# Eight dense chunks in every image group, six indirect transfers under way, reordered first loads, border taps without padding

## The chip, the core and the metric

The kernel runs on one core of a Trainium2 chip. A core has five engines that run side by side and meet only at semaphores: TensorE (PE in the profile; its weight loads are listed as PEld), VectorE (DVE), ScalarE (ACT), GpSimd (POOL) and SyncE (SP), and 16 DMA engines that all queues share. The metric is device time in microseconds from the start to the end of one execution. The kernel before the change takes 2309.76 us in the median of 14 runs (2300.69 to 2324.23 us).

## The reference, cut to what matters

The input is 32 images of 128 channels and 56 x 56 pixels (3136 tokens). Each image goes through a binary 3 x 3 convolution with padding 1, then a linear attention, then a mixture of 8 experts of which each token uses the best two.

```python
x = x + conv(sign(groupnorm(x)), sign(w)) * Alpha            # layer 0; w from M, Z and rv
t = to_tokens(x)
n = layernorm(t)
q, k, v = n @ Wq + bq, n @ Wk + bk, n @ Wv + bv
t = t + q * sum(k * v, axis=tokens)                           # attention
n = layernorm(t)
probs = softmax(n @ router_w + router_b)
top_p, top_i = top_k(probs, 2)                                # renormed to sum 1
t = t + sum_k top_p[k] * (n @ expert_w[top_i[k]] + expert_b[top_i[k]])
out = from_tokens(t)
```

## The kernel before

**Tiling of one image.** The 3136 tokens of an image are cut into 25 chunks of at most 128 (`n_ck`), and the chunks into blocks of four (`PER`, 512 tokens). The convolution of an image is seven tiles of eight image rows (`conv`, L597 to L608): nine taps accumulate in one PSUM tile of 8 x 56 = 448 columns, reading `xs`, a 58 x 58 bf16 copy of the signs with a border of zeros. After it come the turn to tokens (`to_tokens`, L628), the statistics, a Gram matrix (L703), a chain of eight small steps (`kv_1` to `kv_8`), the projection (`project`, L822) and the routing, most of it small DVE work.

**Two ways through the experts.** The first `DENSE[g]` chunks of an image are *dense*: a block is turned to channels (`to_channels`, L1078), and for each of the eight experts the gates of all tokens are broadcast by DMA over the partitions (`spread`, tile `bc`, L1096), multiplied in on DVE (`gated`, L1105, two experts at a time), and put through the expert on PE (`experts`, L1123, tile `ff`, with the expert biases by L1117). `finish` (L1134) adds, `store` writes out.

The other chunks are *sorted*. Each token is a row of 132 numbers; POOL writes the 128 rows of a chunk into a DRAM table sorted by the pair of experts they need (`scatter`, L1325, one indirect DMA a chunk). When all images of a group have scattered, lists of tiles are made (`list_1` to `list_4`), and for each *quad* of four tiles SP loads the rows (`tile_load`, L1617), PE turns them (`tile_turn`, L1624) and runs just the two experts of the tile (`tile_experts`, L1642), ACT scales both results out of PSUM (`tile_read`, L1660 and L1667), DVE adds (`tile_sum`, `tile_out`), and the result goes to DRAM (`tile_store`). Then POOL gathers each chunk's rows back (`gather`, L1400, one indirect DMA a chunk), PE turns a block of them (`back_turn`, L1415), ACT copies (`back_out`, L1423) and SP stores.

Images 0 to 27 are in four groups, `GROUPS = (8, 8, 8, 4)`, with `DENSE = (8, 8, 12, 12)` dense chunks an image; images 28 to 31 are dense in all 25 chunks. So the kernel runs 96 dense blocks, 428 scatters, 428 gathers and 132 quads.

**What limits the indirect transfers.** `in_turn` makes each indirect DMA wait until the one issued `IN_FLIGHT = 4` places earlier has landed. All scatters and gathers go through POOL in one order.

**The order of the work.** A planner (`in_order`) decides it. Every step is entered with `at(due, key, engine, work, ...)`: a due time, an engine, an estimate of its work, the steps it comes after, the buffers it takes and frees (`ROOM`), and `delay`, the time until what it started has landed. The planner plays the steps through on these estimates and emits them in the order found; PE, DVE and ACT then execute exactly that order, so a step that is late holds up everything behind it on its engine. For scatters and gathers the estimate is 2.0 on POOL, and a gather is taken to land after `GATHER_LANDS = 12.0`.

**The start.** SP issues the first image's load (`load_x`, L308 and L309) and then some 20 small loads of weights and biases (L322 to L335); ACT issues `rv`, `M` and the five `Z` (L318 to L321). DVE sums `M` and `Z` in five steps over all 1152 columns (L340), ACT takes the sign (L343, tile `w_bin`). These stand ahead of the planned steps. `gn_sum` (ACT, L547) sums the first image, `gn_total`, `gn_mean` (L560) and `gn_neg` make its mean, `gn_sign` (L567) writes `xs`, and the first convolution follows. `prepare` centres the weights after the first image's convolution. SP issues the loads of images 1 and 2 behind the small loads.

Of the kernel before, what the change touches and what calls it, by code (L numbers as in the profile page):

```python
# [48 lines left out]
AF = mybir.ActivationFunctionType  # L49
ALU = mybir.AluOpType  # L50
# [4 lines left out]
C = 128  # L55
GROUP = 4
TAPS = 9
K_REP = 5
N_EXP = 8
# [4 lines left out]
ROWS = 8  # L64
# [2 lines left out]
ROW = C + 4  # L67
N_PAIR = N_EXP * (N_EXP - 1) // 2
GROUPS = (8, 8, 8, 4)
DENSE = (8, 8, 12, 12)  # L70

IN_ORDER = {mybir.EngineType.PE, mybir.EngineType.DVE, mybir.EngineType.Activation}
NEWTON = 3
IN_FLIGHT = 4

GATE_LANDS, SPREAD_LANDS, STORE_LANDS, TILE_LANDS, GATHER_LANDS = 5.0, 6.5, 5.0, 6.0, 12.0
TILE_PACE = (0.7, 0.6, 0.4, 0.3)
GATHER_PACE = (1.0, 0.8, 0.5, 0.4)
N_Q = C + 2 * N_EXP
# [11 lines left out]
    x=3, tok=3, ps=5, acc=1, ff=2, y=3, qs=3, tt=4, bc=4, gt=2, gated=2,  # L91
# [86 lines left out]
def conv_attn_moe_kernel(  # L178
# [19 lines left out]
    nc = tc.nc  # L198
# [121 lines left out]
    for k in range(K_REP):  # L320
        nc.scalar.dma_start(z_sb[k], z_w[k].rearrange("i t o -> i (t o)"))  # L321
    nc.sync.dma_start(alpha_col, alpha.rearrange("c a b -> c (a b)"))  # L322
    nc.sync.dma_start(wq_sb, w_q)
    nc.sync.dma_start(wk_sb, w_k)
    nc.sync.dma_start(wv_sb, w_v)
    nc.sync.dma_start(bq_col, b_q.unsqueeze(1))
    nc.sync.dma_start(bq_bc, b_q.unsqueeze(0).to_broadcast([C, C]))
    nc.sync.dma_start(bk_bc, b_k.unsqueeze(0).to_broadcast([C, C]))
    nc.sync.dma_start(bv_bc, b_v.unsqueeze(0).to_broadcast([C, C]))
    nc.sync.dma_start(rw_sb, router_w)  # L330
    nc.sync.dma_start(rb_bc, router_b.unsqueeze(0).to_broadcast([C, N_EXP]))
    nc.sync.dma_start(ew_s.rearrange("d (e c) -> d e c", c=C), expert_w.rearrange("e d c -> d e c"))
    nc.sync.dma_start(eb_row, expert_b.rearrange("e c -> (e c)").unsqueeze(0))
    for r in range(9):
        nc.sync.dma_start(eb9[r * N_EXP : (r + 1) * N_EXP, :], expert_b)  # L335


    w_acc = z_sb[K_REP]
    for k in range(K_REP):
        nc.vector.scalar_tensor_tensor(  # L340
            w_acc, z_sb[k], rv_bc[:, k : k + 1], w_acc, ALU.mult, ALU.add
        )
    nc.scalar.activation(w_bin.rearrange("p t o -> p (t o)"), w_acc, AF.Sign)  # L343

    wv_bk = const.tile([C, C], F32, name="wv_bk")
    n_bkbv = const.tile([C, C], F32, name="n_bkbv")
# [174 lines left out]
    def plan_image(i: int):  # L521
# [15 lines left out]


        def load():
            d["x"] = load_x(i, nc.sync) if i else first_x  # L540

        def gn_sum(r0, r1):
            if r0 == 0:
# [22 lines left out]
        def gn_sign(r0, r1):  # L566
# [5 lines left out]
            )  # L572

        at(
            s - 60, ("load", i), "SP", 0.1, load,
            after=[("load", i - 1)] + ([("gn_sign", 0, GN_PARTS - 1)] if i == 1 else []),
            take=["x"], delay=13.0 if i else 19.0,
        )
        for j in range(GN_PARTS):
            rows = j * height // GN_PARTS, (j + 1) * height // GN_PARTS  # L580
# [15 lines left out]

        def conv(b):  # L597
            cv = ps.tile([C, ROWS, width], F32, tag="ps", name=f"cv_{i}_{b}")
            for t in range(TAPS):
                dy, dx = t // 3, t % 3  # L600
                nc.tensor.matmul(  # L601
                    cv,
                    lhsT=w_bin[:, t, :],
                    rhs=xs[:, b * ROWS + dy : b * ROWS + dy + ROWS, dx : dx + width],
                    start=(t == 0),
                    stop=(t == TAPS - 1),
                )
            d["cv", b] = cv  # L608

# [1211 lines left out]
```

## Time and profile before

| what | us |
|---|---|
| median of 14 runs | 2309.76 |
| the profiled execution | 2322.44 |
| its span | 2320.7 |
| PE busy | 2121.9 (91%), 12074 instructions |
| PE weight loads busy | 1458.3 (63%) |
| DVE busy | 1980.0 (85%) |
| ACT busy | 1528.0 (66%) |
| POOL busy | 1000.4 (43%) |
| DMA bytes | 448.56 MB, 193 GB/s mean |
| granted TensorE clock, mean | 0.963 |

Times below are from the start of the span of this one execution, which is 0.5% above the median. "Busy" of PE counts the stretches in which any matmul is under way; matmuls overlap, so the distance from one group's start to the next is the better price of a matmul. A row of a timeline or of the chain gives the start, the duration and the engine, line and tiles; in brackets stands the idle time before it and what ended it. A wait row says who waited for whom: total, times, longest.

### The profile page before, as it was taken

The numbers are of one execution on the slowest core, as the hardware profiler recorded it, in microseconds if no ns is written. First come the engines' busy times: TensorE is split into PE (matmuls) and PEld (weight loads), VectorE is DVE, ScalarE is ACT, GpSimd is POOL, SyncE is SP. The second block draws the span as 40 slices with busy tenths as digits, with TensorE's granted clock in tenths as the row PEclk, the third lists the DMA queues.
The fourth block names the chain that finished last, engine by engine and source line by source line (L and its number), as shares of the span: only waits on it lengthen the run. The fifth ranks groups of instructions, "written<-read, shape, count | busy, mean of one in ns | idle before, by whom it ended". The sixth has DMA issues, their size and how long they took to land. (4 is left out here: it accounts for less than half of the span.)

```text
span 2320.7 us, 45155 instructions
## 1 busy us (share of the span) xinstructions
PE 2121.9 (91%) x12074; PEld 1458.3 (63%) x12074; DVE 1980.0 (85%) x6360; ACT 1528.0 (66%) x4883; POOL 1000.4 (43%) x971
## 2 busy tenths in 40 slices
PE   4989899999999999889999999998889879999989
PEld 2656556666777776557667776655567655666644
DVE  3799999999999999898788989898678868778875
ACT  3766767668888887467867887555567846674311
POOL 1044444333332335554545454544545345534564
PEclk9999999999999999899999999999899989999999
DMA  4044454465665665457767876565666766877788
GB/s 166 29 138 159 161 178 154 138 180 180 187 174 178 179 182 184 135 168 235 214 184 228 257 212 205 183 213 171 213 207 197 229 170 197 266 227 236 233 281 304
DMA packets 317741, 448.56 MB, mean 193 GB/s; under 512 B 61066, under 2 KB 223154, under 8 KB 317491
## 3 DMA queue, kind: packets, MB, share of 16 engines
q1 hardware_dynamic: 289090, 386.97, 53.4%
q0 software_dynamic: 27392, 55.17, 7.9%
q10 hardware_dynamic: 1008, 3.54, 0.4%
q8 instruction: 102, 1.67, 0.3%
q14 instruction: 149, 1.21, 0.2%
HBM read 319.51 MB, written 126.00 MB: 192 GB/s over the span
## 5 line engine op out<-in xcount | busy, mean ns | idle before, releaser
L1325 POOL DMA_INDIRECT rows<-tok,row_no x428 | 501.2, 1171 | 786.7 <-ACT tok L1319 389.7
L1123 PE MATMUL ff<-gated,ew_d 128*128 128x512 f32 (+1 forms) x1536 | 721.9, 599 | 37.9 <-DVE gated L1105 25.1
L1400 POOL DMA_INDIRECT back<-res,res_no x428 | 489.7, 1144 | 518.4 <-PE back_ps L1415 171.4
L1105 DVE TENSOR_TENSOR gated<-tt,bc 128x1024 f32<-128x1024 f32 x384 | 450.2, 1177 | 96.5 <-PE ff L1123 46.5
L1123 PEld LDWEIGHTS ff<-gated,ew_d 128*128 128x128 f32 x1536 | 278.0, 195 | 278.5 <-issue 216.8
L601 PE MATMUL cv<-xs,w_bin 128*128 128x448 bf16 x2016 | 427.5, 361 | 9.5 <-ACT xs L567 4.2
L1660 ACT ACTIVATE v<-to,t_in 128x128 f32<-128x128 f32 x528 | 252.6, 478 | 122.7 <-PE to L1642 54.3
L601 PEld LDWEIGHTS <-w_bin 128*128 128x128 bf16 x2016 | 199.1, 100 | 188.1 <-issue 36.4
L1642 PEld LDWEIGHTS to<-ew_s,turned 128*128 128x128 f32 x2112 | 258.4, 193 | 49.3 <-issue 32.2
L1642 PE MATMUL to<-ew_s,turned 128*128 x2112 | 271.9, 278 | 18.2 <-issue 10.3
L836 ACT ACTIVATE qs<-q,r 128x136 f32<-128x136 f32 (+1 forms) x800 | 246.3, 407 | 54.2 <-PE q L822 33.7
L694 ACT ACTIVATE y<-tok,r 128x128 f32<-128x128 f32 (+1 forms) x800 | 252.5, 405 | 39.5 <-DVE r L512 21.4
L822 PE MATMUL q<-move,x 128*128 128x144 f32 (+1 forms) x1600 | 246.0, 301 | 23.2 <-issue 11.4
L822 PEld LDWEIGHTS q<-move,x 128*128 128x128 f32 (+1 forms) x1600 | 219.0, 197 | 54.3 <-issue 25.4
L703 PEld LDWEIGHTS gram<-y 128*128 128x128 f32 (+1 forms) x1600 | 198.6, 191 | 34.0 <-issue 22.2
L641 DVE BATCH_NORM_STATS2 st<-tok 128x6 f32<-128x128 f32 (+1 forms) x800 | 179.2, 277 | 42.3 <-ACT tok L634 34.3
L703 PE MATMUL gram<-y 128*128 128x129 f32 (+1 forms) x1600 | 210.5, 277 | 0.0
L1667 ACT ACTIVATE w<-to,t_in 128x128 f32<-128x128 f32 x528 | 205.6, 389 | 0.0
L856 DVE BATCH_NORM_STATS2 st<-tok 128x6 f32<-128x128 f32 (+1 forms) x800 | 194.8, 281 | 0.0
L634 ACT COPY tok<-xt 128x512 f32<-128x512 f32 (+1 forms) x224 | 117.6, 566 | 105.1 <-PE xt L628 51.8
L612 DVE SCALAR_TENSOR_TENSOR x<-cv,alpha_col,x 128x448 f32<-128x448 f32 x224 | 151.3, 676 | 32.7 <-PE cv L601 21.0
L1319 ACT ACTIVATE tok<-tok,a 128x128 f32<-128x128 f32 (+1 forms) x428 | 173.5, 436 | 0.1
(216 smaller groups left out, 2883.1 us busy)
## 6 DMA issues: line engine op xcount, KB each, us to landing
bc<-gp SPq DMA_DIRECT2D x368, 512.0 KB
x<-in_x_dram SPq DMA_DIRECT2D x64, 784.0 KB
t_in<-rows SPq DMA_DIRECT2D x528, 66.0 KB
res<-v SPq DMA_DIRECT2D x132, 256.0 KB
out_dram<-o SPq DMA_DIRECT2D x100, 256.0 KB
out_dram<-tt SPq DMA_DIRECT2D x92, 256.0 KB
rows<-zeros SPq DMA_DIRECT2D x116, 66.0 KB
rows<-tok,row_no POOLq DMA_INDIRECT x428
```

Source lines behind the costliest of these rows:

```text
L601: nc.tensor.matmul(cv, lhsT=w_bin[:, t, :], rhs=xs[:, b * ROWS + dy : b * ROWS + dy + ROWS, dx : dx + width], start=(t == 0), stop=(t == T ...
L694: nc.scalar.mul(y[:n, j, :C], d["tok"][:n, c, :C], d["r1"][:n, c : c + 1])
L703: nc.tensor.matmul(d["gram"], lhsT=y[:n, j, :C], rhs=y[:n, j, :], start=(c == 0), stop=(c == n_ck - 1),)
L822: nc.tensor.matmul(p[:n, k, :], lhsT=d["x"][:, c * C : c * C + n], rhs=move, start=True, stop=True,)
L836: nc.scalar.mul(qs[:n, k, : C + N_EXP], p[:n, k, : C + N_EXP], d["r1"][:n, c : c + 1])
L1105: nc.vector.tensor_tensor(g[:, :, :n], d["tt", b][:, :n].unsqueeze(1).to_broadcast([C, 2, n]), d.pop(("bc", b, k))[:, :, :n], ALU.mult,)
L1123: nc.tensor.matmul(d["ff", b][:, :n], lhsT=ew_d[:, e * C : (e + 1) * C], rhs=g[:, j, :n], start=False, stop=(e == N_EXP - 1),)
L1325: dma = nc.gpsimd.indirect_dma_start(out=groups[group]["rows"], out_offset=bass.IndirectOffsetOnAxis(ap=d["row_no"][:n, c - n_dense : c - ...
L1400: dma = nc.gpsimd.indirect_dma_start(out=d["back", c][:n, :], out_offset=None, in_=groups[group]["res"][: quads_of(group) * WIDE, :], in_o ...
L1642: nc.tensor.matmul(p[:, k, j, :], lhsT=t[:, n * C : (n + 1) * C], rhs=ew_s[:, bass.ds(d["cols", q][j][n], C)], start=True, stop=True,)
L1660: nc.scalar.activation(d["v", q][:, n, :], p[:, k, 0, :], AF.Identity, bias=row[:, C + 2 : C + 3], scale=row[:, C : C + 1],)
L1667: nc.scalar.mul(d["w", q][:, n, :], p[:, k, 1, :], row[:, C + 1 : C + 2])
```

## The change

`DENSE` becomes (8, 8, 8, 8): in the 12 images of the last two groups a third block of four chunks goes the sorted way. `IN_FLIGHT` becomes 6, the planner's estimate for a scatter or gather 1.5 in place of 2.0, and `GATHER_LANDS` 9.0 in place of 12.0. The convolution takes the centre tap first and each border tap only over the columns and rows where it meets the image, so the zero border of `xs` is no longer read. The weight sum is cut into three parts of 384 columns, it and the sign become planned steps, and the convolution waits for the last part (`("binary", 2)`). The small loads move from SP to POOL (`load_small`, a planned step), `prepare` waits for them, and the loads of images 1 and 2 move from SP to ACT.

```diff
-DENSE = (8, 8, 12, 12)
+DENSE = (8, 8, 8, 8)
...
-IN_FLIGHT = 4
-GATE_LANDS, SPREAD_LANDS, STORE_LANDS, TILE_LANDS, GATHER_LANDS = 5.0, 6.5, 5.0, 6.0, 12.0
+IN_FLIGHT = 6
+GATE_LANDS, SPREAD_LANDS, STORE_LANDS, TILE_LANDS, GATHER_LANDS = 5.0, 6.5, 5.0, 6.0, 9.0
...
-    nc.sync.dma_start(wq_sb, w_q)
...
-    for r in range(9):
-        nc.sync.dma_start(eb9[r * N_EXP : (r + 1) * N_EXP, :], expert_b)
+    def load_small():
+        nc.gpsimd.dma_start(wq_sb, w_q)
...
+        for r in range(9):
+            nc.gpsimd.dma_start(eb9[r * N_EXP : (r + 1) * N_EXP, :], expert_b)
...
-    for k in range(K_REP):
+    def weight_sum(k, part):
+        cols = slice(part * 3 * C, (part + 1) * 3 * C)
         nc.vector.scalar_tensor_tensor(
-            w_acc, z_sb[k], rv_bc[:, k : k + 1], w_acc, ALU.mult, ALU.add
-        )
-    nc.scalar.activation(w_bin.rearrange("p t o -> p (t o)"), w_acc, AF.Sign)
+            w_acc[:, cols], z_sb[k][:, cols], rv_bc[:, k : k + 1], w_acc[:, cols], ALU.mult, ALU.add
+        )
+    def binary(part):
+        cols = slice(part * 3 * C, (part + 1) * 3 * C)
+        nc.scalar.activation(w_bin.rearrange("p t o -> p (t o)")[:, cols], w_acc[:, cols], AF.Sign)
...
-            d["x"] = load_x(i, nc.sync) if i else first_x
+            d["x"] = load_x(i, nc.scalar if i < 3 else nc.sync) if i else first_x
...
-            s - 60, ("load", i), "SP", 0.1, load,
+            s - 60, ("load", i), "ACT" if 0 < i < 3 else "SP", 0.9 if 0 < i < 3 else 0.1, load,
...
-            take=["x"], delay=13.0 if i else 19.0,
+            take=["x"], delay=7.0 if i == 1 else 13.0,
...
-            for t in range(TAPS):
+            for n, t in enumerate((4, 0, 1, 2, 3, 5, 6, 7, 8)):
                 dy, dx = t // 3, t % 3
+                r0, r1 = int(b == 0 and dy == 0), ROWS - int(b == n_conv - 1 and dy == 2)
+                c0, c1 = int(dx == 0), width - int(dx == 2)
                 nc.tensor.matmul(
-                    cv,
+                    cv[:, r0:r1, c0:c1],
                     lhsT=w_bin[:, t, :],
-                    rhs=xs[:, b * ROWS + dy : b * ROWS + dy + ROWS, dx : dx + width],
-                    start=(t == 0),
-                    stop=(t == TAPS - 1),
+                    rhs=xs[:, b * ROWS + dy + r0 : b * ROWS + dy + r1, dx + c0 : dx + c1],
+                    start=(n == 0),
+                    stop=(n == TAPS - 1),
                 )
...
-                + [("conv", i, b - 1) if b else ("conv", i - 1, n_conv - 1), ("weights",)],
+                + [("conv", i, b - 1) if b else ("conv", i - 1, n_conv - 1), ("binary", 2)],
...
-                s + 140 + 2 * k, ("scatter", i, c), "POOL", 2.0, scatter, c,
+                s + 140 + 2 * k, ("scatter", i, c), "POOL", 1.5, scatter, c,
...
-                    due + each * k / n_sort, ("gather", i, c), "POOL", 2.0, gather, c,
+                    due + each * k / n_sort, ("gather", i, c), "POOL", 1.5, gather, c,
...
-    at(0.0, ("weights",), "SP", 0.1, lambda: None, delay=24.0)
-    at(30.0, ("prepare",), "PE", 6.0, prepare, after=[("conv", 0, n_conv - 1)])
+    for k in range(K_REP):
+        at(0.0, ("weights", k), "SP", 0.01, lambda: None, delay=9.5 + 2.2 * k)
+        for part in range(3):
+            at(
+                float(k), ("weight_sum", k, part), "DVE", 0.5, weight_sum, k, part,
+                after=[("weights", k), ("weight_sum", k - 1, part)],
+            )
+    for part in range(3):
+        at(-50.0, ("binary", part), "ACT", 0.45, binary, part, after=[("weight_sum", K_REP - 1, part)])
+    at(5.0, ("small",), "POOL", 20.0, load_small, delay=3.0)
+    at(30.0, ("prepare",), "PE", 6.0, prepare, after=[("conv", 0, n_conv - 1), ("small",)])
```

More of the change, by code (lines that the diff above doesn't have):

```diff
@@ L322, in conv_attn_moe_kernel @@
     nc.sync.dma_start(alpha_col, alpha.rearrange("c a b -> c (a b)"))
-    nc.sync.dma_start(wq_sb, w_q)
[L324 to L333, printed above, removed]
-    for r in range(9):
-        nc.sync.dma_start(eb9[r * N_EXP : (r + 1) * N_EXP, :], expert_b)
+    def load_small():
+        nc.gpsimd.dma_start(wq_sb, w_q)
+        nc.gpsimd.dma_start(wk_sb, w_k)
+        nc.gpsimd.dma_start(wv_sb, w_v)
+        nc.gpsimd.dma_start(bq_col, b_q.unsqueeze(1))
+        nc.gpsimd.dma_start(bq_bc, b_q.unsqueeze(0).to_broadcast([C, C]))
+        nc.gpsimd.dma_start(bk_bc, b_k.unsqueeze(0).to_broadcast([C, C]))
+        nc.gpsimd.dma_start(bv_bc, b_v.unsqueeze(0).to_broadcast([C, C]))
+        nc.gpsimd.dma_start(rw_sb, router_w)
+        nc.gpsimd.dma_start(rb_bc, router_b.unsqueeze(0).to_broadcast([C, N_EXP]))
+        nc.gpsimd.dma_start(ew_s.rearrange("d (e c) -> d e c", c=C), expert_w.rearrange("e d c -> d e c"))
+        nc.gpsimd.dma_start(eb_row, expert_b.rearrange("e c -> (e c)").unsqueeze(0))
+        for r in range(9):
+            nc.gpsimd.dma_start(eb9[r * N_EXP : (r + 1) * N_EXP, :], expert_b)
     w_acc = z_sb[K_REP]
-    for k in range(K_REP):
+    def weight_sum(k, part):
+        cols = slice(part * 3 * C, (part + 1) * 3 * C)
         nc.vector.scalar_tensor_tensor(
-            w_acc, z_sb[k], rv_bc[:, k : k + 1], w_acc, ALU.mult, ALU.add
+            w_acc[:, cols], z_sb[k][:, cols], rv_bc[:, k : k + 1], w_acc[:, cols], ALU.mult, ALU.add
         )
-    nc.scalar.activation(w_bin.rearrange("p t o -> p (t o)"), w_acc, AF.Sign)
+    def binary(part):
+        cols = slice(part * 3 * C, (part + 1) * 3 * C)
+        nc.scalar.activation(
+            w_bin.rearrange("p t o -> p (t o)")[:, cols], w_acc[:, cols], AF.Sign
+        )
     wv_bk = const.tile([C, C], F32, name="wv_bk")
@@ L1765, in conv_attn_moe_kernel @@
         plan_group(g)
-    at(0.0, ("weights",), "SP", 0.1, lambda: None, delay=24.0)
-    at(30.0, ("prepare",), "PE", 6.0, prepare, after=[("conv", 0, n_conv - 1)])
+    for k in range(K_REP):
[6 more added lines that the diff above has]
+    for part in range(3):
+        at(
+            -50.0, ("binary", part), "ACT", 0.45, binary, part,
+            after=[("weight_sum", K_REP - 1, part)],
+        )
+    at(5.0, ("small",), "POOL", 20.0, load_small, delay=3.0)
+    at(30.0, ("prepare",), "PE", 6.0, prepare, after=[("conv", 0, n_conv - 1), ("small",)])
     at(40.0, ("prepare_sorted",), "PE", 1.0, prepare_sorted, after=[("prepare",)])
```

## The prediction, made before the changed kernel ran

> **What bounds the kernel now.** I read the page's busy shares and slices first, then the chain that ended last, then windows and waits of the stretch in which the changed images run.
>
> ```profile
> PE 2121.9 (91%) x12074; PEld 1458.3 (63%) x12074; DVE 1980.0 (85%) x6360; ACT 1528.0 (66%) x4883; POOL 1000.4 (43%) x971
> PE   4989899999999999889999999998889879999989
> ```
>
> PE is busy 91% of the span, and nearly all of it outside the first slice and slices 28 to 33: PE work is what a change must remove. The chain confirms it for the end, and prices PE groups by the distance between starts:
>
> ```profile
> 2269.12 0.44 PE l L1078 x4
> 2269.55 3.44 PE ff L1123 x8
> 2272.99 0.22 PE ff L1117
> ```
>
> Two stretches by engine, then the longest waits of PE and of ACT in the second:
>
> ```profile
> 1000.00:1440.00 440.00, 420.44 (x2549) 303.73 (x2548) 380.46 (x1199) 332.71 (x1060) 225.04 (x193) 0.97 0.68 209
> 1560.00:1920.00 360.00, 309.77 (x1812) 221.77 (x1811) 270.82 (x837) 232.23 (x737) 169.99 (x152) 0.92 0.66 199
> ...
> PE xt L628 <- ACT tok L634: 13.5, 1, 13.5
> ...
> ACT tok L634 <- DMA rows<-tok,row_no: 15.8, 1, 15.8
> ```
>
> After the length the columns are PE, PEld, DVE, ACT and POOL. PE is busy 96% of the first stretch but 86% of the second (309.77 of 360). Its largest stall there comes from POOL: a scatter landed late, so a token buffer came free late.
>
> **Dense to sorted, on PE.** Twelve blocks leave the dense way, one in each of images 16 to 27. A dense block costs 16 expert matmuls (8 in 3.44) 6.88, the bias 0.22, the turn to channels 0.44: 7.54 us. A sorted block is one more quad (132 to 144), priced in PE's timeline:
>
> ```profile
> 704.95 0.60 PE L1624 MATMUL turn<-ident,t_in 128*128 128x128 f32 x4
> 705.39 1.06 PE L703 MATMUL gram<-y 128*128 128x129 f32 x8
> ...
> 708.00 1.95 PE L1642 MATMUL to<-ew_s,turned 128*128 x16
> 709.79 1.06 PE L703 MATMUL gram<-y 128*128 128x129 f32 x8
> ```
>
> From start to start: turn 0.44, experts 1.79, and 0.44 again to turn the gathered rows back: 2.67. Four more chunks lengthen `places`: L1254 takes 6.65 us in seven images with 17 sorted chunks and 5.89 in eight with 13, so 0.21 an image; with its other matmuls, 0.3. Net 7.54 - 2.67 - 0.3 = 4.57 a block, 55 us in all. Where PE already waits, less PE work is not less time, so I take PE's share of the weaker stretch, 0.86: **-47 us**. Bounds: -28 (half of it lost in waits) and -80 (all 55, and half of the second stretch's 50 us of PE idle gone too).
>
> **The same blocks elsewhere**, beside PE. DVE loses four `gated` of 1.21 (445.6 / 368) and a `finish` of 0.68, gains two adds of 0.69 and six steps over 17 instead of 13 chunks (0.64 at 17, so 0.15 each): -3.2 a block, -39 us. ACT loses a copy of 0.59, gains 4 row adds of 0.41, copies of 0.62 and 0.60, 4 reads of 0.48 and 4 of 0.39: +5.7 a block, +69 us; at 65% of the second stretch it has room, and where its reads are late PE waits for PSUM, which the 0.86 covers. DMA loses per block four broadcasts of 512 KB, 72 KB of gates, a 256 KB store, and gains 264 KB of scatter, 264 of tile loads, three times 256 of results, gathers and stores: -1.1 MB, -13 of 448.6 MB. SP's number of issues hardly changes (4 tile loads and a store of results in, 7 gate loads out). I count nothing for these; if ACT had no room, its 69 us would eat the gain.
>
> **POOL** gains 48 scatters and 48 gathers of 1.17 busy (62.03 / 53) plus 0.30 between two: +141 us on 1000. It is one queue: scatters stand behind gathers, token buffers wait for scatters, back turns for gathers. Windows of the gathers alone, a wait, and two rows of POOL's timeline:
>
> ```profile
> 1948.00:2206.00 258.00, 121.23 (x104) 0.97 0.77 233
> 2206.00:2306.00 100.00, 62.03 (x53) 0.95 0.91 311
> ...
> POOL back L1400 <- PE back_ps L1415: 117.2, 28, 18.2
> ...
> 2303.26 0.94 POOL L1400 DMA_INDIRECT back<-res,res_no  x1 [1.17 <-DMA back<-res,res_no]
> ```
>
> The last two groups' gathers run at 2.48 and 1.89 us each, 2.28 over all. In the first window most waiting is for buffers that PE's back turns free, in the second for landing. In the trace's DMA packets the last gathers end 5 to 6.5 us after their start, and the fourth later one starts about 1.1 us after that: (6 + 1.1) / 4 = 1.8 a gather. Six under way make it 1.2, below the floor of 1.47, so 1.5 to 1.6 should be reached, if the latency stays.
>
> Now the end. Groups 2 and 3 will have 204 gathers, not 156. They start when group 2's quads are stored. The quads start about 65 us earlier (eight blocks of 7.2, and start and taps) but are 40, not 32; at the 8.4 us of now (270 / 32) that gives the same 1948, at 7.5 some 1912. I take 1930. With 12 us behind the last gather, as now, 1930 + 204 x 1.6 + 12 = 2268, where PE's work alone would end at 2321 - 62 = 2259. So I add **+8 us** for the gather chain; bounds 0 and that of the rivals.
>
> The Trainium skill, in "DMA: Bandwidth & Descriptors", section "Anatomy of one DMA", gives 2.0 us plus bytes / 436e3 for a POOL transfer, for 64 KB an estimate of 2.15 us. By it four under way would suffice at 0.54 us each, and raising the limit would be worth nothing; the 5 to 6.5 us above, on a loaded chip, decide against it.
>
> **Border taps.** 63 matmuls an image, nine in 1.72 us (next groups' starts, 42.39 to 44.11), so 0.43 ns a column. Six taps lose a column of 56 in 8 rows (48), and in two of seven tiles three lose a row: 95 of 4032 columns, 2.4% of 224 x 1.72 = 385 us, 9 us; by 0.86, **-8 us**. No row shows a PSUM tile written in pieces of 55: bounds -9 and 0, the latter if each broken row costs the column that it saves. Reading pieces of 56 from rows of 58 already costs no more than contiguous 512 columns (0.43 for two passes).
>
> **The start.**
>
> ```profile
> 23.09 1.42 DVE L340 SCALAR_TENSOR_TENSOR z<-z,rv_bc 128x1152 f32<-128x1152 f32 x1 [1.33 <-DMA z<-in_L_conv_Z_dram]
> 30.22 7.58 PE L601 MATMUL cv<-xs,w_bin 128*128 128x448 bf16 x27 [1.01 <-ACT xs L567]
> 58.87 0.59 PE L560 MATMUL gm_ps<-ch_sum,group_w 128*128 128x1 f32 x2 [4.56 <-DVE ch_sum L556]
> ```
>
> The last `Z` lands at 23, the first convolution follows 7.1 us later. Between 14 and 16 us ACT's queue moved 28 KB a us, before that 370, while SP's small rows went through. With these on POOL, 20 issues at POOL's pace, `Z` may land between 17.4 (1.24 MB left at 14, at 370) and 23. Behind it come three parts (1.42 / 3 each) 1.5, the last sign 0.45, six sums of the image that now stand behind the signs (0.70 each) 4.2, and 1.8 as now: 8.0. Convolution at 25.4 to 31, I take 27: -3. Then PE waits 4.56 for the second image's sums and 2.84 more for its signs, though its load landed around 32: the sums were planned behind `prepare`. Now that load is issued by ACT behind the signs, about 33 us, and lands by 39; the sums fit into ACT's idle time before `prepare`. I take 4 of the 7.4: **-7 us** for the start, bounds +2 and -12. POOL's 20 issues end near 30 and their data is needed at 46; the memsets of `prepare_sorted` behind them wait harmlessly. If POOL took 2 us an issue, `prepare` would slip some 5 us.
>
> In the same page's section "Issuing engines are not separate DMA queues" the skill says that another issuing engine saves just issue time. By that rule `Z` still lands at 23, the start is worth -4 and the sum is 3 us less. No row can yet say which.
>
> **Sum:** -47 - 8 - 7 + 8 = -54. The profiled execution, 2322.4 with a span of 2320.7, stands 0.55% above the median, so I subtract from the median: 2309.8 - 54 = 2256 us.
>
> **Rivals.** (a) *The gather chain sets the end.* For: the floor of 1.47 leaves little room, and 117 us of its waiting now is for PE's order, which more transfers under way do not mend. Against: its plan (1.5 a gather, landing after 9) now orders back turns earlier. At 1.75 from 1930: 2299 of span, 2285 median. (b) *Slower: the same chain at today's pace and start.* At 2.0 from 1948: 1948 + 408 + 12 = 2368, 2355 median; the point from which it decides is (2321 - 12 - 1948) / 204 = 1.77 us a gather. Against it stands only the latency argument above. (c) *Stalls go too:* -80 in place of -47 and no gather term, 2309.8 - 95 = 2215.
>
> **How the numbers follow.** The forecast has 0.50 (2235 to 2275), (a) 0.22 (2275 to 2303), (b) 0.17, (c) 0.06, and 0.05 is left for a balance at no change. A measurement here tells 0.3%, about 7 us, from nothing. Faster 0.50 + 0.22 + 0.06 = 0.78, same 0.05, slower 0.17. The range 2228 to 2308 holds the forecast, (a) and most of the balance.
>
> **What would show it.** PE busy near 2060 us, L1123 x1344 instead of x1536, L1642 x2304, DVE near 1940, ACT near 1600, POOL near 1140. The last 200 gathers at 1.5 to 1.6 us; PE above 90% in its last 100 us if the forecast holds, well below with `back_ps` waiting for `back` if (a) or (b) does. First convolution at 25 to 28, and no gap of 7 us before the second. Wrong would make it: gathers that still wait for PE's turns, quads that do not start 65 us earlier, or in-order waits of PE growing with ACT's added reads.

## The result, and the profile after

The changed kernel takes 2371.44 us in the median of 10 runs (2355.97 to 2381.58), the kernel before on the same chip 2310.76 us. The ratio is 1.0263, with a 95% interval of 1.0238 to 1.0288: 2.6% slower, where 2.3% faster was forecast. The profiled execution took 2358.1 us, with a span of 2356.4 us at a mean granted clock of 0.950 (before: 2320.7 at 0.963). It is one of the shorter ones: the two profiled spans differ by 35.7 us, the medians by 60.7, so the page shows some six tenths of the loss.

First the page of the changed kernel, busy time and PE's slices:

```profile
PE 2088.1 (89%) x12148; PEld 1458.6 (62%) x12148; DVE 1950.3 (83%) x6346; ACT 1570.7 (67%) x5041; POOL 1088.9 (46%) x1087
PE   5898999998999998889998998867888889899878
```

Two things are to be seen. DVE went down and ACT and POOL went up, as forecast in sign: DVE by 29.7 us (39 were forecast), ACT by 42.7 (69), POOL by 88.5 (141 with the gaps between its transfers). But PE busy fell by 33.8 us only, and the part of the span in which PE is idle rose from 198.8 to 268.3 us. These two, -33.8 and +69.5, are the 35.7 us by which the span grew.

The matmuls themselves did become fewer as forecast. By the groups of the two profiles: the dense experts went from 721.9 to 630.6 us (x1536 to x1344), the bias rows by -3.6, the turns to channels by -6.0, the sorted experts from 271.9 to 296.8 (x2112 to x2304), the turns of tiles by +7.6, of gathered rows by +9.5, the sorting matmuls by +6.1. That is -52.8 us, where the prediction said -55. The taps took some 5 us more away, as an experiment below shows. That leaves some 24 us of the 58 that did not come off PE's busy time. Groups with as many matmuls as before grew: the convolution from 427.5 to 432.5 us, the turns to tokens (`xt`) from 122.3 to 133.1. The clock accounts for most of this. The trace's clock record has only full and half speed, and PE was busy in the stretches at half speed for 123.7 us before and 159.6 after. Half of that would have been enough at full speed, so an estimate of 18 us more was lost (79.8 against 61.8).

Where the idle time came in shows in the windows of the changed kernel (length, then PE, PEld, DVE, ACT and POOL busy, the granted clock, the DMA share, GB/s):

```profile
1000.00:1440.00 440.00, 404.07 (x2543) 298.21 (x2542) 375.02 (x1221) 342.61 (x1104) 234.20 (x210) 0.97 0.65 194
1440.00:1560.00 120.00, 86.97 (x452) 57.98 (x451) 87.67 (x330) 49.26 (x161) 71.93 (x69) 0.84 0.51 153
1560.00:1920.00 360.00, 298.16 (x1797) 220.08 (x1798) 262.18 (x840) 249.14 (x794) 186.82 (x168) 0.90 0.59 177
2100.00:2300.00 200.00, 173.22 (x801) 108.83 (x801) 154.50 (x364) 76.17 (x233) 117.47 (x103) 0.94 0.80 257
```

PE's idle time in these stretches, before and after: 19.6 and 35.9, 8.8 and 33.0 (PE was busy 111.16 of these 120 us before), 50.2 and 61.8, 15.8 and 26.8 us. The added idle time is spread: 63 of the 69.5 us fall into these four stretches, none has more than 25 us of it. The worst of them also has the lowest granted clock (0.84 between 1440 and 1560, where it was 0.97).

The waits of PE between 1000 and 1920 us in the changed kernel (total, times, longest):

```profile
PE xt L642 <- ACT tok L648: 14.7, 2, 11.4
PE q L836 <- issue: 14.4, 8, 5.3
PE gram L717 <- ACT y L708: 10.4, 4, 5.7
PE turn L1638 <- DMA t_in<-rows: 8.4, 4, 7.5
```

The largest wait of the kernel before, for a token buffer (13.5 us), is still there (14.7 in two), and others as large stand beside it. Behind it stands ACT's copy of tokens, which writes the buffer. Its waits that ended with a transfer of POOL, in the same stretch:

```profile
ACT tok L648 <- DMA rows<-tok,row_no: 14.8, 4, 6.2
ACT tok L648 <- DMA back<-res,res_no: 12.1, 1, 12.1
```

Together they are 26.9 us, where the kernel before had one of 15.8. (The copy needs scatters only. The gather that the second row names was issued 1.2 us after a scatter, and their landings cannot be told apart there.) No single wait carries the loss, so experiments had to tell which of the added work makes them.

The end of the chain is dense expert work, as before:

```profile
2330.85 3.44 PE ff L1137 x8
2335.67 3.70 PE ff L1137 x8
```

### The profile page after: what moved, and what is told of

Its sections match the earlier page's. It is cut to its first block, busy times and chain, and to the rows that moved or that the text cites. A ratio compares the mean times of both kernels' runs of the same rounds, so it can differ in the third digit from the quotient of the medians.

```text
span 2356.4 us, 45685 instructions
## 1 busy us (share of the span) xinstructions
PE 2088.1 (89%) x12148; PEld 1458.6 (62%) x12148; DVE 1950.3 (83%) x6346; ACT 1570.7 (67%) x5041; POOL 1088.9 (46%) x1087
## 5 line engine op out<-in xcount | busy, mean ns | idle before, releaser
L1339 POOL DMA_INDIRECT rows<-tok,row_no x476 | 541.3, 1137 | 774.2 <-ACT tok L1333 434.8
L1414 POOL DMA_INDIRECT back<-res,res_no x476 | 527.1, 1107 | 472.0 <-issue 125.7
L1137 PE MATMUL ff<-gated,ew_d 128*128 128x512 f32 (+1 forms) x1344 | 630.6, 599 | 32.7 <-DVE gated L1119 20.1
L1119 DVE TENSOR_TENSOR gated<-tt,bc 128x1024 f32<-128x1024 f32 (+1 forms) x336 | 392.5, 1173 | 113.0 <-PE ff L1137 39.8
L615 PE MATMUL cv<-xs,w_bin 128*128 128x440 bf16 (+3 forms) x2016 | 432.5, 364 | 23.3 <-ACT xs L578 10.7
L1137 PEld LDWEIGHTS ff<-gated,ew_d 128*128 128x128 f32 x1344 | 244.1, 196 | 243.8 <-issue 200.4
L1674 ACT ACTIVATE v<-to,t_in 128x128 f32<-128x128 f32 x576 | 279.4, 487 | 154.4 <-PE to L1656 49.9
L1656 PEld LDWEIGHTS to<-ew_s,turned 128*128 128x128 f32 x2304 | 282.9, 194 | 56.4 <-issue 30.9
L1656 PE MATMUL to<-ew_s,turned 128*128 x2304 | 296.8, 279 | 18.5 <-ACT tok L648 6.5
L836 PEld LDWEIGHTS q<-move,x 128*128 128x128 f32 (+1 forms) x1600 | 216.8, 197 | 62.7 <-issue 30.6
L862 DVE TENSOR_TENSOR tok<-tok,qs 128x384 f32<-128x384 f32 (+1 forms) x288 | 148.6, 516 | 44.9 <-ACT qs L850 21.1
```

The costliest lines, as they stand in the source:

```text
L615: nc.tensor.matmul(cv[:, r0:r1, c0:c1], lhsT=w_bin[:, t, :], rhs=xs[:, b * ROWS + dy + r0 : b * ROWS + dy + r1, dx + c0 : dx + c1], start= ...
L836: nc.tensor.matmul(p[:n, k, :], lhsT=d["x"][:, c * C : c * C + n], rhs=move, start=True, stop=True,)
L1119: nc.vector.tensor_tensor(g[:, :, :n], d["tt", b][:, :n].unsqueeze(1).to_broadcast([C, 2, n]), d.pop(("bc", b, k))[:, :, :n], ALU.mult,)
L1137: nc.tensor.matmul(d["ff", b][:, :n], lhsT=ew_d[:, e * C : (e + 1) * C], rhs=g[:, j, :n], start=False, stop=(e == N_EXP - 1),)
L1339: dma = nc.gpsimd.indirect_dma_start(out=groups[group]["rows"], out_offset=bass.IndirectOffsetOnAxis(ap=d["row_no"][:n, c - n_dense : c - ...
L1414: dma = nc.gpsimd.indirect_dma_start(out=d["back", c][:n, :], out_offset=None, in_=groups[group]["res"][: quads_of(group) * WIDE, :], in_o ...
```

## The experiments

The question: which part of the change costs the time, and why does a kernel with less work on PE, its busiest engine, take longer? **Theory A:** POOL's one queue of indirect transfers sets the pace of images 16 to 27. Each scatter or gather that is added holds token buffers and results longer, and PE waits for them. **Theory B:** PE, ACT and DVE lose by the new order and the added ACT work, and POOL has nothing to do with it. The expectations of the parts alone use other letters: there B stands for the shorter estimates in the plan and C for the new start. Every ratio is against the kernel before on the same chip. The kernel before itself took 2246 to 2325 us on the chips used, so only ratios are compared, and small differences between ratios from different chips are not read.

### One part at a time

The dense edit alone:

```diff
-DENSE = (8, 8, 12, 12)
+DENSE = (8, 8, 8, 8)
```

> Alone on the kernel before: DENSE = (8, 8, 8, 8). Theory A (the sorted way overloads the one queue of scatters and gathers, so token buffers come free late and PE waits): slower by itself, 2.0 to 4.0% (2357 to 2402 us), with PE idle near 270 us against 199, most of the growth between 1400 and 1950 us, although PE's work falls by about 55 us. Theory B (the shorter estimates in the plan are what makes PE wait) and theory C (the new start and the order that follows from it do): faster by itself, 1 to 2% (2264 to 2287 us).

Measured: 1.0326 [1.0308, 1.0343], slower by itself, as theory A has it. PE is idle for 243.8 us, where 270 were expected.

Six transfers under way alone:

```diff
-IN_FLIGHT = 4
+IN_FLIGHT = 6
```

> Alone on the kernel before: IN_FLIGHT = 6. The order of all engines stays as it is. All theories: within 0.5% or a little faster (2295 to 2315 us); gathers of the last 100 us at about 1.5 us each in place of 1.9. If more transfers under way delay the other DMA traffic, slower by up to 1%.

Measured: 0.9956 [0.9940, 0.9973]. One sentence of the expectation was wrong. In the traces PE and ACT run the same instructions in the same order as before (DVE but for two), but at 146 of the 856 places in POOL's order a scatter stands where a gather stood, or the reverse. Only PE, DVE and ACT are bound to the planner's order; POOL's came out different when only the waits between transfers were changed.

The new estimates alone:

```diff
-... TILE_LANDS, GATHER_LANDS = 5.0, 6.5, 5.0, 6.0, 12.0
+... TILE_LANDS, GATHER_LANDS = 5.0, 6.5, 5.0, 6.0, 9.0
-("scatter", i, c), "POOL", 2.0        # and ("gather", i, c)
+("scatter", i, c), "POOL", 1.5
```

> Alone on the kernel before: the planner's estimates, 1.5 for a scatter or gather and 9.0 until a gather has landed; still four under way. Theory B: slower by 1.5 to 3% (2345 to 2380 us), PE waiting for rows that are turned back or for token buffers. Theories A and C: within 0.7% (2294 to 2326 us).

Measured: 0.9974 [0.9953, 0.9995].

The new start alone (the changed kernel with the old values of all of the above, and with the old taps):

```diff
-    nc.sync.dma_start(wq_sb, w_q)
+    nc.gpsimd.dma_start(wq_sb, w_q)
...
-    at(0.0, ("weights",), "SP", 0.1, lambda: None, delay=24.0)
+    for k in range(K_REP): ... weight_sum in three parts, binary in three parts
```

> Alone on the kernel before: the new start (weight sum in parts and planned, small loads on POOL, the loads of images 1 and 2 on ACT). The first convolution starts about 6 us earlier and image 2's is about 15 us earlier. Theory C: slower by 1 to 3% (2333 to 2380 us), since the shifted start changes the order in the middle. Theories A and B: faster by 0.2 to 0.7% (2294 to 2306 us).

Measured: 0.9962 [0.9943, 0.9982], some 8.5 us by the ratio.

The border taps alone:

```diff
-            for t in range(TAPS):
+            for n, t in enumerate((4, 0, 1, 2, 3, 5, 6, 7, 8)):
...
-                    cv,
+                    cv[:, r0:r1, c0:c1],
```

> Border taps alone. By the prediction's term (8 to 9 us of PE's columns): ratio 0.996 to 0.997. If broken rows cost as much as the columns they save: 1.000. If a PSUM tile written in pieces costs PE time or shifts waits, and is what made the changes without the dense edit 1.2% slower together: 1.005 to 1.015.

Measured: 0.9971 [0.9933, 1.0009]. The convolution's row of this kernel:

```profile
L604 PE MATMUL cv<-xs,w_bin 128*128 128x440 bf16 (+3 forms) x2016 | 422.2, 359 | 6.8 <-ACT xs L567 4.2 <-DVE own L1277 1.8 <-ACT w L1670 0.5
```

It was 427.5 us with a mean of 361 ns before: 5.3 us of busy time, at a clock of 0.966 against 0.963. Taken alone, then, only the dense edit loses. Everything else gives 0.3 to 0.4% each.

The changed kernel without the dense edit:

```diff
-DENSE = (8, 8, 8, 8)
+DENSE = (8, 8, 12, 12)
```

> The changed kernel with DENSE = (8, 8, 12, 12) again, all its other edits kept. If the other edits only add up (0.4, 0.3 and 0.4% measured alone, and 0.3% at most for the taps): faster than before by 1.0 to 1.5%. If they only help or hurt together with the eight dense chunks: within 0.5% of before.

Measured: 1.0123 [1.0017, 1.0228]. This did not fit: four parts that gain one by one lose together. So the whole loss is not the dense edit's: of the 2.6% some 1.2% (0.2 to 2.3) is there without it. It is taken up further below.

### Is it POOL's queue?

The dense edit alone shows on the spot what a late scatter does. From its timeline (start, duration, engine, line, tiles; in brackets the idle time before and what ended it):

```profile
1298.72 1.00 POOL L1325 DMA_INDIRECT rows<-tok,row_no  x1 [0.30 <-issue]
1303.47 0.96 POOL L1400 DMA_INDIRECT back<-res,res_no  x1 [3.75 <-DMA rows<-tok,row_no]
1304.73 0.91 POOL L1400 DMA_INDIRECT back<-res,res_no  x1 [0.30 <-issue]
1305.94 0.94 POOL L1325 DMA_INDIRECT rows<-tok,row_no  x1 [0.30 <-issue]
1310.94 1.07 ACT L634 COPY tok<-xt 128x512 f32<-128x512 f32 x2 [12.07 <-DMA rows<-tok,row_no]
1311.56 1.64 DVE L641 BATCH_NORM_STATS2 st<-tok 128x6 f32<-128x128 f32 x8 [11.21 <-ACT tok L634]
1311.58 3.52 PE L601 MATMUL cv<-xs,w_bin 128*128 128x448 bf16 x9 [11.09 <-ACT tok L634]
```

Two gathers stand ahead of an image's last scatter. The first of them waits 3.75 us, because four transfers are under way, so the scatter starts at 1305.94 and lands some 5 us later. Until then ACT cannot write the next image's tokens (a token buffer is free only when the scatters of the image three before it have landed), and DVE and PE, each in its own order, wait 11 us behind it. POOL does no more than 1 us of work at a time here; it is the order and the landing that hold the others. The first matmuls behind the gap also take longer: the nine here take 3.52 us, against 1.89 for nine at 1294.29. The trace's clock record has half speed from 1303.5 to 1317.1, so they run in it.

To count it, the gathers were taken off POOL, once with and once without the dense edit:

```diff
-            dma = nc.gpsimd.indirect_dma_start(out=d["back", c][:n, :], ... res_no ...)
+            nc.sync.dma_start(d["back", c][:n, :], groups[group]["res"][fixed row :][:n, :])
```

> DENSE = (8, 8, 8, 8) as the only edit of the change, but every gather is a plain load of 128 result rows issued by SP (it takes rows of a fixed place, so the tokens get back other tokens' results); POOL keeps only the scatters. Compared with the next kernel. Theory A: with POOL relieved the PE work removed turns into time: 1.5 to 2.5% faster than the same kernel with DENSE = (8, 8, 12, 12). Rival (ACT's added reads set the pace): still slower than it, by 1 to 3%.

Measured: 0.9754 [0.9706, 0.9802].

> The kernel before with every gather as a plain load of 128 result rows issued by SP (the tokens get back other tokens' results). The pair to the kernel above. Theory A: faster than before by 1 to 4%, since POOL also holds it up, but less than it helps the kernel above. Rival: within 1%.

Measured: 0.9693 [0.9646, 0.9741]. With the gathers on SP the dense edit costs 0.9754 / 0.9693, 0.6% (2249.03 to 2262.84 us), instead of 3.3%. For the pair neither expectation came true: it is not 1.5 to 2.5% faster, and not 1 to 3% slower. The planner gave both kernels an order of their own, since it now plays the gathers on SP, so part of the difference could be that order. PE's windows with the dense edit, gathers on SP:

```profile
1000.00:1440.00 440.00, 418.31 (x2685) 309.47 (x2684) 405.06 (x1344) 359.17 (x1161) 130.82 (x115) 0.99 0.69 207
1560.00:1920.00 360.00, 330.15 (x2085) 244.43 (x2084) 284.38 (x826) 280.15 (x882) 62.42 (x57) 0.98 0.72 208
```

PE is busy 95% and 92% there at a clock of 0.98 to 0.99, where the dense edit with gathers on POOL has 400.01 of 440 and 300.37 of 360 us, at 0.96 and 0.92. Without the dense edit, gathers on SP, it has 429.22 and 345.86.

The reverse test leaves all dense blocks as they were and adds only transfers:

```diff
             alone(f"rows{group}", dma, in_turn(dma))
+            if 16 <= i < 28 and c < n_dense + 8:
+                more = nc.gpsimd.indirect_dma_start(out=groups["spare"], ... same rows ...)
+                alone("spare", more, in_turn(more))
```

> The kernel before, and in each of images 16 to 27 eight of the thirteen scatters are sent a second time into a spare tensor that nobody reads (96 more POOL transfers in all, as many as the dense edit adds; dense blocks, quads, gathers and all other work stay as they were). Theory A (POOL's one queue, with few under way, paces the images): the extra transfers take a turn of about 2.1 us each, 200 us of queue, part of it in slack, and no PE work goes in exchange, so it is slowed at least as much as by the dense edit: ratio 1.03 to 1.06. Theory B (the dense edit loses through the new order of PE's, ACT's and DVE's work, not through POOL): the order of those engines is unchanged here, ratio 0.995 to 1.010.

Measured: 1.0317 [1.0268, 1.0365], as much as the dense edit. 96 transfers that nobody needs cost 73 us (2306.40 to 2379.62), 0.76 us each, in a program in which POOL is busy 45% of the span. Its windows and two waits between 1000 and 1920 us:

```profile
1000.00:1440.00 440.00, 395.30 (x2374) 288.50 (x2373) 351.42 (x1088) 307.12 (x975) 245.35 (x221) 0.94 0.64 200
1560.00:1920.00 360.00, 307.24 (x1741) 217.21 (x1741) 269.14 (x868) 225.20 (x715) 199.65 (x183) 0.91 0.63 198
...
PE xt L628 <- ACT tok L634: 19.8, 2, 10.5
...
ACT tok L634 <- DMA rows<-tok,row_no: 30.6, 3, 14.0
```

ACT's wait for landed scatters, 15.8 us before, is 30.6, and PE waits behind it. In the two traces PE, DVE and ACT run the same instructions in the same order (12074, 6360 and 4883), so theory B cannot explain this run. Nor are the DMA engines fuller: their share is 0.64 and 0.63, where it was 0.68 and 0.66. What the added transfers do through their number and what through POOL's order is not separated: scatters and gathers changed places here too, at 68 of 856. That POOL's transfers alone can cost as much as the dense edit is shown; where the 73 us arise is shown only in part, some 15 of them by the row above.

### What is left without POOL

Scatters and gathers both as plain SP transfers:

```diff
-            dma = nc.gpsimd.indirect_dma_start(out=groups[group]["rows"], ... row_no ...)
+            dma = nc.sync.dma_start(groups[group]["rows"][fixed row :][:n, :], d["tok"][:n, c, :])
...
-            nc.sync.dma_start(t[:, k, :], d["rows"][bass.ds(row, C), :])
+            nc.sync.dma_start(t[:, k, :], d["rows"][fixed row :][:C, :])
```

> Dense edit alone, and neither scatters nor gathers go over POOL: SP stores token rows in plain order, loads tiles from fixed rows of that store and loads results from fixed rows. Tokens so meet other experts and get other tokens' results; bytes, matmuls and every step of PE, ACT and DVE stay. To be read against the next run. If POOL's queue alone stood between the 55 us of PE work and the time: 0.98 times the time of the next run or less. If the new order of PE, DVE and ACT, or their work, also eats it: 0.995 to 1.01 times the time of the next run.

Measured: 1.0050 [1.0031, 1.0069], to be read with the next.

> The kernel before with the same replacement of scatters and gathers by plain SP transfers of fixed rows (same part of the computation left out). If transfers over POOL cost time in the kernel before, too: ratio 0.95 to 0.97 (gathers alone gave 0.969). If scatters cost nothing more: 0.969.

Measured: 0.9991 [0.9979, 1.0003]. Neither expectation for this kernel alone came true. For the pair the second one did: the dense edit costs 0.6% again (1.0050 / 0.9991), with no transfer of rows on POOL. So POOL is not all: the 55 us of PE work are not gained even then. In this pair PE's busy time falls by 29.7 us and its idle time grows by 38.0; in the pair with the gathers alone on SP it is 26.9 and 42.4. Two waits of PE between 1000 and 2200 us, with the dense edit:

```profile
PE turn L1615 <- DMA t_in<-rows: 42.6, 26, 5.4
PE ff L1123 <- DVE gated L1105: 21.5, 19, 5.3
```

Without the edit the same two are 9.1 and 41.3 us. PE then waits for tiles loaded by SP instead of for gated tokens. The first wait grows in the pair with the gathers alone on SP as well, from 2.7 to 21.7 us, though SP issues 428 or 476 transfers fewer there. Why the tiles come late (SP's queue, the buffers that they need, or ACT's 50 us more of work) was not separated. That the kernel before gained nothing here, while it gained 3% from moving the gathers alone, is a comparison between two chips (2246 and 2325 us for the kernel before), and no run tells whether SP's extra load or the chip makes the difference.

The opposite step in size:

```diff
-DENSE = (8, 8, 12, 12)
+DENSE = (8, 8, 16, 16)
```

> The opposite step in size: sixteen dense chunks in groups 2 and 3 instead of twelve, nothing else. PE work grows by 12 x 4.57 = 55 us, POOL loses 96 transfers. If the 0.8 us that an extra transfer cost (73 us for 96) is also saved by one less: 2306 + 55 - 73, ratio 0.985 to 1.0. If the kernel before already waits little for POOL in these images, so that only PE's work counts: ratio 1.015 to 1.03.

Measured: 1.0055 [1.0036, 1.0075], between the two expectations. 55 us of added PE work cost 12 us by the ratio, 15 by the medians; the rest came back from waits and from the clock (0.98 in each run, 0.97 in the kernel before on that chip). PE in this kernel is busy 120.00 of 120 us between 1440 and 1560, and 349.96 of 360 after 1560, at a clock of 1.00. On this side of twelve chunks PE sets the pace in these stretches; on the other it idles.

### Six under way, and the estimates

> Before with DENSE = (8, 8, 8, 8) and IN_FLIGHT = 6, nothing else; the order of the engines is that of the kernel with the dense edit alone. Theory A (the one queue of indirect transfers sets the pace): the 38 us at the end, in which only gathers run, shrink by 20 us or more, and the token copies wait less for scatters: 1.010 to 1.020 of before in place of 1.033. Rival (ACT's added reads, 69 us, set the pace): PE's idle time between 1050 and 1850 us stays as it is, only the end shrinks, 1.020 to 1.028.

Its edit is `IN_FLIGHT = 6` on top of the dense edit. Measured: 1.0580 [1.0519, 1.0642]: both expectations were wrong, since six under way made the kernel with the dense edit slower, not faster. PE, DVE and ACT run the same instructions in the same order as with the dense edit alone (1.0326), so what six under way add lies with POOL's transfers. With the new estimates on top of that:

> Dense edit, six under way and the planner's new estimates for scatters and gathers. The dense edit alone gave 1.033, with six under way 1.058. If the estimates are what gives the changed kernel back what the six under way cost: 1.02 to 1.035. If they do nothing: 1.05 to 1.06.

Measured: 1.0340 [1.0277, 1.0402]. With the start and the taps it is the 1.0263 of the whole change; the difference is about what they gave alone, but the two ratios come from two chips. The whole change with four under way:

```diff
-IN_FLIGHT = 6
+IN_FLIGHT = 4
```

> The whole change but with four transfers under way. If six under way hurt beside the dense edit, as they did without the other edits (1.058 against 1.033): faster than the changed kernel's 1.026, 1.00 to 1.015. If what hurt there was POOL's order of that one build: 1.025 or more.

Measured: 1.0191 [1.0152, 1.0231]; the expected 1.00 to 1.015 was too good, but it is below the 1.0263 of six. Six under way did not help beside the dense edit in either pair, each of two chips.

Then the four parts that did not add. Start and six under way:

> New start and six transfers under way, nothing else. If the gains of the two alone (0.9962 and 0.9956) add: 0.992. If POOL's order, sorted anew each time, decides by itself how the images wait, they do not add: anywhere from 0.995 to 1.015.

Measured: 0.9971 [0.9937, 1.0005]: no loss, and hardly the sum (0.992). Six under way and the new estimates:

> Six under way and the new estimates of scatters and gathers (1.5 and 9.0), nothing else. If their gains alone (0.9956 and 0.9974) add: 0.993. If this pair is why the four parts together lost 1.2% (start and taps giving some 0.7% back): 1.015 to 1.02.

Measured: 1.0135 [1.0091, 1.0180]. This is the pair that does not add. PE, DVE and ACT run the order that they have with the estimates alone (0.9974), so this loss, too, comes by POOL. POOL's waits between 1000 and 1920 us in it:

```profile
POOL back L1400 <- PE back_ps L1415: 132.1, 25, 15.6
POOL rows L1325 <- ACT tok L1319: 97.5, 26, 10.6
```

The first is 29.7 us with six under way alone and 43.9 with the estimates alone; in the changed kernel without the dense edit it is 139.2. Gathers stand at the head of POOL's queue and wait for PE to empty their buffers, and the scatters wait behind them. The two edits together put gathers too far ahead; each by itself does not. That it is the order, and not the number under way, is argued from these waits: no run changes POOL's order alone.

The start and the taps together, without the rest:

> New start and border taps, nothing else: four under way, the old estimates, the old dense blocks. If their gains alone (0.9962 and 0.9971) add: 0.993, faster than both kernels. If this pair is why the four parts together lost 1.2%: 1.005 to 1.02.

Measured: 0.9931 [0.9905, 0.9956], 2291.54 against 2310.09 us: the gains add, and it is faster than both kernels.

## Why the prediction was wrong, point by point

**Dense to sorted, -47 us: this step failed.** The count of PE work was right (-52.8 of -55 by the groups). What failed is "where PE already waits, less PE work is not less time, so I take PE's share of the weaker stretch, 0.86", with bounds of -28 and -80. The factor took the waits as given and asked how much of the gain they leave. But the edit adds to what makes the waits: 96 transfers in a queue on which token buffers, results and PE's order depend. The bound should have reached above zero. Alone the edit measured +3.3%, +71 us on its chip (2253.10 to 2324.01); 96 such transfers with no edit measured +73. Between the -47 and the +71 lie 118 us. With the gathers off POOL the edit cost 14 us, so about half of the 118 goes with POOL's transfers. The other half, the gain that does not come even then, shows in part as PE waiting for the tiles of the quads (some 19 and 34 us more in the two pairs without gathers on POOL); its cause stays open. The prediction put ACT's 69 us, SP and the tile loads at nothing, and no run separates them.

**POOL, +141 us: seen, and priced at the wrong place.** The prediction wrote that scatters stand behind gathers and that token buffers wait for scatters, quoted the wait of 15.8 us, and then charged the queue only at the end, for the last 204 gathers. In images 16 to 27 it charged nothing beyond the 0.86. POOL's busy share of 43 to 47% hid this: each transfer occupies it for 1.1 us, but holds a place among four and a buffer until it lands.

**The clock: not in the sum at all.** A long wait of PE costs twice here, once as idle time and once in the work behind it. The granted clock fell from 0.963 to 0.950; in PE's busy time that is the estimate of 18 us above. The Trainium skill says in "TensorE: Matmul & The Clock Gate", Part 1, that the array falls to half its clock after an idle window of about 3.4 us and comes back after a busy one. The profile agrees in kind: the trace's clock record shows stretches at 0.5 of 3.4 to 13.7 us, 173.0 us in all before and 233.5 after, PE's idle time in them included.

**The gather chain at the end, +8 us: wrong start and pace, no effect.** The row of the gathers of groups 2 and 3 in the changed kernel (count, min/median/max duration in ns, first and last start):

```profile
L1414 POOL DMA_INDIRECT back<-res,res_no x204: 906/947/2420, 1983.5 to 2340.9; - x102
```

They started at 1983.5 instead of 1930 and took 357.4 / 203, 1.76 us each, instead of 1.6. The quads of group 2 came 24 us earlier, not 65 (first turn at 1622.7 instead of 1646.8), and at the 8.4 us each of before, so that the last result of the group was stored 52 us later (1980.0 instead of 1927.7). But PE's largest waits from 1983 on are 9.8 us for nothing that the profile shows and 8.0 for gated tokens, none for gathered rows; POOL waits for PE (60.9 us behind `back_ps`). The chain ends in PE's expert work. PE is busy only 81% of the last 100 us, the sign named for (a) and (b), but without the wait for `back` that belongs to it. Of the rivals, (b) gave a time close to the measured one, 2355, by luck: its mechanism did not act, since the gathers did not set the end. (a) fails on the same row, (c) on PE's idle time. With the dense edit alone and four under way PE does wait for gathered rows there, 18.3 us in 23 waits; in the changed kernel, with six, no such wait is among the largest. The figure that the Trainium skill gives in "DMA: Bandwidth & Descriptors", section "Anatomy of one DMA", an estimate of 2.15 us in the prediction, is too short for most transfers of this trace: the scatter above landed some 5 us after its start, and by the DMA packets of the kernel before, matched to the transfers in order, the median scatter takes 3.3 us from its start to its last packet (a tenth take 1.9 or less).

**Border taps, -8 us: right in sign, too large.** 5.3 us of PE's busy time alone, ratio 0.9971 with an interval that holds both -8 us and nothing. The rows tell more: a tile in the middle of an image and the last one, each with the group that follows (changed kernel):

```profile
33.40 1.89 PE L615 MATMUL cv<-xs,w_bin 128*128 128x448 bf16 x9
35.13 0.60 PE L642 MATMUL xt<-ident,x 128*128 128x128 f32 x4
...
37.73 1.82 PE L615 MATMUL cv<-xs,w_bin 128*128 128x448 bf16 x9
39.39 0.41 PE L372 MATMUL centred<-wq_sb,centre 128*128 128x128 f32 x2
```

From start to start the middle tile takes 1.73 us, as before (1.72), though six of its nine taps have 440 columns instead of 448. The last tile takes 1.66: there three taps lose a whole row as well. So a lost row saves time and a lost column does not, the condition that the prediction gave for its bound of nothing. In the median of the tiles at full clock it is 1.726 us before; with the taps alone it is 1.731 in the five middle tiles and 1.660 in the two outer ones. That is 0.11 us an image, an estimate of 3.4 us in all instead of 9.

**The start, -7 us: right in the sum, not in its parts.** The changed kernel's rows:

```profile
21.41 1.15 DVE L345 SCALAR_TENSOR_TENSOR z<-z,rv_bc 128x384 f32<-128x384 f32 x2 [1.21 <-DMA z<-in_L_conv_Z_dram]
24.32 6.64 PE L615 MATMUL cv<-xs,w_bin 128*128 128x448 bf16 x27 [3.47 <-ACT xs L578]
54.25 7.01 PE L615 MATMUL cv<-xs,w_bin 128*128 128x448 bf16 x27 [0.90 <-ACT xs L578]
```

The last `Z` came at 21.4 instead of 23.1, the first convolution at 24.3 instead of 30.2 (27 was taken), the second at 54.3 instead of 62.3. The two waits ahead of it are 3.91 and 0.90, where they were 4.56 and 2.84; the prediction took them to be gone but for 3.4. The first convolution came 2.9 us after the last `Z`, where the prediction had 8.0: the image's sums did not stand behind the signs, the group mean is computed at 20.3. So the convolution gave more than forecast (-5.9 instead of -3) and the two waits less (-2.6 instead of -4). Alone the start measured -8.5 us. The rule of the Trainium skill in "DMA: Bandwidth & Descriptors", section "Issuing engines are not separate DMA queues", by which `Z` would still have landed at 23, holds better than the row of 17.4: with the small loads on another engine `Z` came 1.7 us earlier.

**Six under way and the estimates, nothing in the sum outside the gather chain: this failed too.** The pace was right or better: the last 100 gathers start 1.28 us apart in the median (1.58 before), below the 1.47 taken for a floor, which came from a mean of 1.17 us a gather, where the changed kernel's median is 0.947. But POOL's order changed with the two edits, which the prediction did not foresee. Together they cost 1.35%. Without the dense edit the change measured +1.2% (1.0123, with a wide interval), where taps and start alone make -15 us, or -0.6%, in the prediction's sum.

## What to carry to other kernels

A queue that is busy 45% can still set the pace, if buffers are held until its transfers land and others execute in order behind them: price an added transfer in the stretch where it is added, by the waits it lengthens (0.76 us of time each here), and let the bound go beyond zero. When an edit trades work of the busiest engine for transfers, adding the transfers alone is the cheapest test, because it needs none of the edit. Small edits to limits and estimates of a planned program need not add: two that gained 0.4 and 0.3% lost 1.4% together, while two that touch separate places (the start and the taps) did add.

## What had not been expected of the hardware

PE's long waits almost always went with a low clock. Of PE's waits of 3 us or more, all 11 in the kernel before and 16 of 17 in the changed one held a stretch at half clock or were followed by one within 3 us. Half of PE's busy time in such stretches, an estimate of what it loses, is 33.1 us with the gathers off POOL (2240 us of span), 61.8 before, 79.8 after and 99.7 with the dense edit and six under way (2460 us); some of what looks like a longer matmul is this.

A matmul that reads rows of 55 instead of 56 columns was no faster in these traces, one with a row of 56 less was: the taps of 440 columns start about as far apart as those of 448 (1.731 against 1.726 us for nine).

The same program is 3.5% apart between chips: the kernel before took 2246, 2253, 2306, 2310, 2311 and 2325 us in the medians on the chips used. No run shows what makes the difference.
